# Gated layers: a tile's values moved to the step after its weights' transposes, ahead of the first scores

## The chip, the cores and the metric

The kernel runs on one core of a Trainium2 chip. The metric is the device time of one execution in microseconds (us). All times in this document are microseconds unless they are marked ns. The core has five engines with a queue of instructions each: TensorE (PE, with its weight loads shown apart as PEld), VectorE (DVE), ScalarE (ACT), GpSimd (POOL) and SyncE (SP), which here only issues DMA transfers. An engine takes its instructions in the order of its queue, and an instruction that waits for a semaphore holds up all that stand behind it.

## The reference

Two sequences of 2048 tokens with 256 features pass through four layers, each added to the stream. The second one, `_L0_ffn_ref`, is the one that matters here: two gated layers of local attention and a gated feed-forward part (FFN). Cut to its core:

```python
def _layer(x, wqkv, qs, ksc, wo, lg, lb, w1, b1, w2, b2):
    h = shift_token(x)                     # second half of the features from the token before
    q, k, v = split(h @ wqkv)              # 8 heads of 64
    q, k = l2norm(q) * qs, l2norm(k) * ksc
    q, k = rotary_xpos(q, k)
    o = local_attention(q, k, v)           # windows of 128: own window and the one before, masked
    x = x + o @ wo
    h = layernorm(shift_token(x)) * lg + lb
    a, g = split(h @ w1 + b1)              # 2 x 682
    return x + (a * gelu(g)) @ w2 + b2
```

## The kernel before

The kernel has three stages, each of which goes over all 4096 tokens: the first attention layer with its own FFN (to about 665 us), the gated layers (about 665 to 2140), and the last stage (to the end). The change touches the second stage only.

**Tiles and groups.** In the gated stage the residual stream `R` lies in SBUF for all tokens. A tile is 128 tokens; there are `NT` = 32 tiles, and four of them (`GT`) make a group of 512 tokens, of which there are 8 (`NG`). Attention goes by tiles, the FFN by groups, and there are `BL` = 2 layers.

**What one tile does** (class `Tile`). Each of these is a method, named as in the source, with the lines at which the profile shows it:

- `project` (matmuls L679) forms q, k and v of the tile in three calls. For q and k, ACT copies the product out of PSUM (`raw`, L689) and squares it (L690), and POOL forms one half of the rotation (`u2`, L695 and L698). For v, ACT copies it (L686).
- `norms`: DVE sums the squares (L710), POOL takes a maximum (L711) and the power -0.5 (`rn`, L713).
- `rotate_mul` and `rotate_add`: DVE forms the other half of the rotation (L718), adds both (L722), and for k multiplies by `rn` (L724).
- `to_features` (transposes L731, ACT copy L733) turns q or k so that the features lie on partitions.
- `scores` (32 matmuls L748, for half of the heads): DVE adds the mask and takes the maximum while it moves the scores out of PSUM (L757), and forms the exponents' shift (L764).
- `exponents` (ACT L775) and `normalise` (DVE L783, L786) make the weights.
- `weights_to_keys` (transposes L795 and L803) turns the weights of one half of the heads. The result goes to SBUF as `PT`, by ACT for half 0 (L799) and by DVE for half 1 (L797), and the rest as `PR` by ACT (L806).
- `swap_values`: two DMAs on SP make `vs`, the tile's v with its halves of 64 rows exchanged. `values` needs it in the matmuls that take `PR`, and the tile after needs it as `prev_vs`.
- `values` (matmuls L820 with `PT`, L832 with `PR`): the product leaves PSUM as `oT`, half by ACT (L840), half by DVE (L841).
- `output` (matmuls L847): DVE adds the product to `R` (L850).

**What one group does** (class `Ffn`). `shifted` issues the DMAs that make `sh`, the second half of the features of `R` moved down by one token; they wait for the `R` of the group's last tile. `normalise` is the layer norm: DVE statistics of `R` (L881) and of `sh` (L882), their aggregate (L883), POOL's variance and power (L93, L95), and eight DVE operations that write `h` (L887). `to_features` transposes `h` (L117, ACT L122), and POOL adds a bias to `R` (L895) and in the last layer a saved input (L899). `hidden` is one of six blocks of the hidden layer (L908, or L917 for the narrow sixth; ACT gelu L921; DVE L922). `output` is the product of one tile of the group (L929) with DVE's addition to `R` (L933). `begin_b` transposes a finished group of `R` for the projections of the layer (L653, ACT L654).

**The order.** The steps are written by hand. `at(step, what, ...)` puts work into a step, and a loop over the steps calls the methods in one fixed order. A tile projects in step t, has its scores in step t + 1 and, before the change, the part named "attend" in step t + 2: `weights_to_keys`, `values` and `output`. So one step holds three tiles: `p` (projects), `q` (scores) and `a` (attends). Three places in the step, `fill[0]` to `fill[2]`, take FFN work of an earlier group: three hidden blocks in each of two steps, then two outputs in each of two steps. Group g's FFN is prepared in step 4(g + 1) + 2 of its layer. PE runs its instructions nearly in the written order. For DVE, ACT, POOL and SP a scheduler may exchange instructions that do not depend on one another, so their queues differ from the written order. PSUM has eight banks that are given out in a ring.

Of the kernel before, what the change touches and what calls it, by code (L numbers as in the profile page):

```python
# [19 lines left out]
NT = NB * SEQ // P  # L20
TPS = SEQ // P
GT = 4
# [23 lines left out]
def kernel(ctx: ExitStack, tc: tile.TileContext, I: dict, out: bass.AP):  # L46
# [86 lines left out]
    def load_qkv(l):  # L133
        w = {}
        w["wqkv"] = T(wB, [P, KC, 3 * BIN], "wqkvB")
        load(w["wqkv"], I["L0_ffn_wqkv"][l].rearrange("(k p) n -> p k n", p=P))
        return w

    def load_wo(l):
        w = {}  # L140
        w["wo"] = T(wB, [P, BIN // P, D], "woB")
        load(w["wo"], I["L0_ffn_wo"][l].rearrange("(k p) n -> p k n", p=P))
        return w

    def load_ffn(l):
        w = {}
        for name in ("ln_g", "ln_b"):
            w[name] = T(wB, [P, KC], name + "B")
            load(w[name], I["L0_ffn_" + name][l].rearrange("(k p) -> p k", p=P))
        w1 = I["L0_ffn_w1"][l].rearrange("(k p) n -> p k n", p=P)  # L150
        w["w1"] = T(wB, [P, KC, 2, 5 * P], "w1B")

        w["w1r"] = T(wB, [P, KC, P], "w1rB")
        nc.gpsimd.memset(w["w1r"], 0.0)
        for h in range(2):
            load(w["w1"][:, :, h, :], w1[:, :, h * BHID : h * BHID + 5 * P])
            r0 = 64 * (1 - h)
            load(w["w1r"][:, :, r0 : r0 + BREM], w1[:, :, h * BHID + 5 * P : (h + 1) * BHID])
        b1 = I["L0_ffn_b1"][l]
        w["b1"] = T(wB, [P, 2, BNC], "b1B")  # L160
        for h in range(2):
            load(w["b1"][:, h, 0:5], b1[h * BHID : h * BHID + 5 * P].rearrange("(k p) -> p k", p=P))
            load(
                w["b1"][0:BREM, h, 5:6],
                b1[h * BHID + 5 * P : (h + 1) * BHID].rearrange("(k p) -> p k", p=BREM),
            )
        w2 = I["L0_ffn_w2"][l]
        w["w2"] = T(wB, [P, BNC, D], "w2B")
        load(w["w2"][:, 0:5, :], w2[0 : 5 * P].rearrange("(k p) n -> p k n", p=P))
        nc.gpsimd.memset(w["w2"][:, 5, :], 0.0)  # L170
        load(w["w2"][0:BREM, 5, :], w2[5 * P : BHID])
        w["b2"] = T(wB, [P, D], "b2B")
        load(w["b2"], bcast_rows(I["L0_ffn_b2"][l], D))
        return w


    with ExitStack() as st_a:
# [284 lines left out]
        def at(step, what, *args):  # L462
            steps.setdefault(step, {}).setdefault(what, []).append(args)
# [5 lines left out]
        for g in range(NG):  # L469
            at(GT * g - 2, "load", g)  # L470
            at(GT * g - 1, "begin", g)
            s = GT * (g + 1) + 2
# [7 lines left out]
        groups, tiles, ffns, done = {0: first_group}, {}, {}, None  # L480
        for s in range(min(steps), max(steps) + 1):
            todo = steps.get(s, {})
            p = a = f = n = q = None
# [3 lines left out]
            if s == GT:  # L487
                weights = {**load_qkv(0), **load_wo(0), **load_ffn(0)}
            if "project" in todo:
                (t,) = todo["project"][0]  # L490
                p = tiles[t] = TileA(t, groups[t // GT])
            if "scores" in todo:
                q = tiles[todo["scores"][0][0]]
            if "attend" in todo:
                a = tiles[todo["attend"][0][0]]
            fill = [lambda x=x: ffns[x[0]].output(x[1]) for x in todo.get("outputs", ())]
            fill += [lambda x=x: ffns[x[0]].hidden(x[1]) for x in todo.get("hidden", ())]
            fill = {0: [], 2: [fill[0:1], fill[1:], []], 4: [fill[0:2], fill[2:3], fill[3:4]]}[len(fill)]
            fill = fill or [[], [], []]
# [84 lines left out]
    with ExitStack() as st_b:  # L584
# [47 lines left out]
        def load_tab(g, sv):  # L632

            tab = T(wb, [P, 4, GT, BHD], "tab")
            t0 = g % GPS * GT
            load(tab, I["rope_b"][:, :, t0 : t0 + GT, :])
            nc.gpsimd.tensor_mul(tab, tab, sv.unsqueeze(2).to_broadcast([P, 4, GT, BHD]))
            return tab
# [304 lines left out]
        for l in range(BL):  # L943
            s0 = l * (NT + GAP)
            for t in range(NT):
                at(s0 + t, "project", l, t)
                at(s0 + t + 1, "scores", l, t)
                at(s0 + t + 2, "attend", l, t)
                if t % GT == 0:
                    at(s0 + t - 2, "tables", l, t // GT)  # L950
                    at(s0 + t - 1, "begin", l, t // GT)
            for g in range(NG):
                s = s0 + GT * (g + 1) + 2
                at(s, "prepare", l, g)
                for c in range(BNC):
                    at(s + 1 + c // 3, "hidden", l, g, c)
                for tt in range(GT):
                    at(s + 3 + tt // 2, "outputs", l, g, tt)
            at(s0 + NT - 1, "free_qkv", l)
            at(s0 + NT + 1, "free_wo", l)  # L960
            at(s0 + NT + 5, "free_ffn", l)

        wts = {0: weights}
        scales = [load_scales(l) for l in range(BL)]
# [1 line left out]
        groups, tiles, ffns = {}, {}, {}  # L966
        sh = None
        for s in range(min(steps), max(steps) + 1):
            todo = steps.get(s, {})
            p = a = q = None  # L970
            if "project" in todo:
                l, t = todo["project"][0]
                if l == BL - 1 and t == GT:
                    load_weights_c()
                p = tiles[l, t] = Tile(l, t, wts[l], tabs[l, t // GT], *groups[l, t // GT], tiles.get((l, t - 1)))
            if "scores" in todo:
                q = tiles[todo["scores"][0]]
            if "attend" in todo:
                a = tiles[todo["attend"][0]]
            fill = [lambda x=x: ffns[x[0], x[1]].output(x[2]) for x in todo.get("outputs", ())]  # L980
            fill += [lambda x=x: ffns[x[0], x[1]].hidden(x[2]) for x in todo.get("hidden", ())]
            for l, g in todo.get("tables", ()):
                tabs[l, g] = load_tab(g, scales[l])
            if "prepare" in todo:
                l, g = todo["prepare"][0]
                f = ffns[l, g] = Ffn(l, g, wts[l])
                sh = f.shifted(sh)
            fill += [lambda: None] * (3 - len(fill))

            if q:  # L990
                q.scores(0)
            if p:
                p.project(0)
            if q:
                q.exponents(0)
            if p:
                p.project(1)
            if q:
                q.scores(1)
            if p:  # L1000
                p.norms()
                p.rotate_mul(0)
                p.project(2)
            if q:
                q.exponents(1)
                q.normalise(0)
            if a:
                a.weights_to_keys(0)
            if p:
                p.rotate_add(0)  # L1010
            fill[0]()
            if a:
                a.weights_to_keys(1)
            if p:
                p.rotate_mul(1)
                p.rotate_add(1)
            if q:
                q.normalise(1)
            fill[1]()
            if a:  # L1020
                a.values()
                a.prev = None
            if q:
                q.swap_values()
            if "prepare" in todo:
                f.normalise()
            if p:
                p.to_features(0)
            fill[2]()
            if p:  # L1030
                p.to_features(1)
            if a:
                a.output()
                tiles.pop((a.l, a.t - 1), None)
            if "prepare" in todo:
                f.to_features()
            for l, g in todo.get("begin", ()):
                groups[l, g] = begin_b(g, groups[l, g - 1][1] if g else None)
            for (l,) in todo.get("free_qkv", ()):
                if l + 1 < BL:  # L1040
                    wts[l + 1] = load_qkv(l + 1)
            for (l,) in todo.get("free_wo", ()):
                if l + 1 < BL:
                    wts[l + 1].update(load_wo(l + 1))
            for (l,) in todo.get("free_ffn", ()):
                if l + 1 < BL:
                    wts[l + 1].update(load_ffn(l + 1))
# [303 lines left out]
```

## Time and profile before

| | us |
|---|---|
| median of 3 runs | 3002.23 |
| lowest and highest | 3000.06 and 3003.87 |
| the profiled execution, own time | 2999.28 |
| its span in the profile | 2997.1 |
| mean granted TensorE clock of it | 0.966 of full speed |
| gated stage, about | 665 to 2140 in the span |

A line of a group or of a wait names the engine, the operation's output and its source line; "L820 <- DVE PT L797" says that the instruction at line 820 waited for the instruction of DVE at line 797 that wrote `PT`. In a timeline a line has the start, the duration, the engine and line, the operation with its shapes, how many of its kind stand together, and in square brackets the idle time before it with what ended it. One group of the first layer, 1001.14 to 1087.36, took 86.22 us, with PE busy for 83.82 of them; one of the second layer, 1564.63 to 1653.50, took 88.87, with PE busy for 84.04.

### The profile page before, as it was taken

What the parts mean: (1) busy time and instruction counts of PE and PEld (TensorE: products, weight loads), DVE (VectorE), ACT (ScalarE), POOL (GpSimd) and SP (SyncE); (2) the same over time, 40 slices, a digit from 0 to 9 for tenths busy, and PEclk for the clock granted to TensorE, in tenths of its full rate; (3) what the DMA queues carried; (4) which work ended last, traced back from release to release, by engine and by line L of the source; (5) the groups of instructions that cost most, each with busy time, mean ns of one, the idle gap of its engine ahead of it and who ended that gap; (6) DMA issues with size and microseconds to landing.
All of it is one profiled execution on the core that took longest, in us unless ns stands there. A gap on an engine that the chain in (4) does not pass through costs nothing.

```text
span 2997.1 us, 50570 instructions
## 1 busy us (share of the span) xinstructions
PE 2738.9 (91%) x20146; PEld 1669.5 (56%) x20146; DVE 1680.5 (56%) x4457; ACT 1150.3 (38%) x2445; POOL 960.3 (32%) x935
## 2 busy tenths in 40 slices
PE   5788888886899999999999999999999999899998
PEld 3555566663566666665656666566544445444554
DVE  6676676634666566665556566555553334643333
ACT  2444444434555555655455555555230000210000
POOL 4443444324433343433344343333410012400001
PEclk8899999998999999999999999999999999999999
DMA  5000000002100101010101101101100000000000
GB/s 153 14 27 26 28 21 19 21 17 72 26 15 23 26 19 26 22 47 24 51 26 29 33 24 25 29 19 26 52 22 0 8 8 7 22 7 4 7 6 13
DMA packets 72763, 78.17 MB, mean 26 GB/s; under 512 B 18685, under 2 KB 57936, under 8 KB 72528
## 3 DMA queue, kind: packets, MB, share of 16 engines
q1 hardware_dynamic: 72528, 74.94, 8.9%
q8 instruction: 159, 2.61, 0.4%
q14 instruction: 76, 0.62, 0.1%
HBM read 42.50 MB, written 8.40 MB: 17 GB/s over the span
## 4 chain that ended last, share of the span: by engine, by line
PE 44%; DVE 18%; POOL 17%; issue 12%; ACT 6%; DMA 2%; SPq 0%; POOLq 0%; ACTq 0%; DVEq 0%
PE ps L1249 14%; POOL rn L713 6%; PE ps L1171 3%; PE ps L908 3%; PE ps L847 3%; DVE S L757 2%; PE ps L447 2%; PE ps L1195 2%; DVE ss L710 2%; POOL u L695 2%; PE ps L1161 2%; POOL S L365 2%; PE ps L439 2%; PE ps L679 2%; POOL rs L95 1%
## 5 line engine op out<-in xcount | busy, mean ns | idle before, releaser
L1249 PE MATMUL ps<-V,s 128*128 128x512 f32 x1024 | 468.3, 593 | 3.2 <-DVE s L1181 3.2
L775 ACT ACTIVATE S<-S,shift,rn 128x192 f32<-128x192 f32 x512 | 274.4, 539 | 168.4 <-DVE shift L764 168.0
L1249 PEld LDWEIGHTS ps<-V,s 128*128 128x128 f32 x1024 | 190.6, 190 | 226.4 <-issue 220.5
L908 PE MATMUL ps<-hT,w1B 128*128 128x512 f32 x640 | 290.3, 598 | 0.6 <-ACT hT L122 0.6
L695 POOL TENSOR_TENSOR u<-raw,tab 128x256 f32<-128x256 f32 x128 | 115.6, 903 | 488.5 <-ACT raw L689 488.4
L679 PE MATMUL ps<-wqkvB,za 128*128 128x512 f32 x384 | 211.9, 634 | 6.1 <-ACT za L654 6.1
L1204 POOL TENSOR_SCALAR veC<-mvC 128x1 f32<-128x1 f32 x32 | 16.6, 517 | 601.4 <-DVE mvC L1202 601.4
L365 POOL TENSOR_TENSOR S<-S,mxA 128x1024 f32<-128x1024 f32 x64 | 121.4, 1897 | 259.1 <-DVE mxA L364 222.8
L1177 DVE SCALAR_TENSOR_TENSOR s<-ps,strip 128x512 f32<-128x512 f32 x128 | 88.4, 691 | 206.8 <-PE ps L1171 206.8
L1192 ACT COPY oCT<-ps 128x512 f32<-128x512 f32 x32 | 18.8, 586 | 466.6 <-PE ps L1190 466.6
L679 PE MATMUL ps<-wqkvB,zb 128*128 128x512 f32 x384 | 197.8, 597 | 0.0
L713 POOL TENSOR_TENSOR rn<-ss,mhalf 128x16 f32<-128x16 f32 x64 | 195.6, 3057 | 5.3
L908 PEld LDWEIGHTS ps<-hT,w1B 128*128 128x128 f32 x640 | 117.4, 193 | 120.2 <-issue 115.1
L757 DVE CUSTOM_DVE_ANT_0 S<-ps,maskB 128x192 f32<-128x192 f32 x512 | 151.5, 351 | 47.0 <-PE ps L748 45.4
L929 PE MATMUL ps<-w2B,hh 128*128 128x256 f32 x768 | 175.5, 379 | 0.0
L439 PE MATMUL ps<-hT,wf 128*128 128x512 f32 x256 | 131.7, 650 | 25.5 <-DVE oT L404 20.2
L929 PEld LDWEIGHTS ps<-w2B,hh 128*128 128x128 f32 x768 | 141.6, 190 | 17.8 <-issue 0.7
L718 DVE TENSOR_TENSOR u<-raw,tab 128x512 f32<-128x512 f32 x128 | 90.7, 709 | 97.6 <-ACT raw L689 95.1
L722 DVE TENSOR_TENSOR u<-u,u 128x512 f32<-128x512 f32 x128 | 92.5, 723 | 88.2 <-POOL u L698 85.9
L786 DVE TENSOR_SCALAR S<-S,rdB 128x192 f32<-128x192 f32 x512 | 138.5, 326 | 2.2
L847 PE MATMUL ps<-woB,oT 128*128 128x256 f32 x512 | 131.1, 395 | 6.5 <-DVE oT L841 5.3
L748 PEld LDWEIGHTS ps<-qkT,qkT 64*64 64x64 f32 x4032 | 99.9, 135 | 65.0 <-issue 63.5
(210 smaller groups left out, 5462.2 us busy)
## 6 DMA issues: line engine op xcount, KB each, us to landing
vs<-v SPq DMA_DIRECT2D x128, 128.0 KB, 2.3
tab<-in_rope_b_dram SPq DMA_DIRECT2D x16, 512.0 KB, 3.9
xg<-in_L_attn_x_dram SPq DMA_DIRECT2D x8, 512.0 KB
xr<-in_L_attn_x_dram SPq DMA_DIRECT2D x8, 512.0 KB, 6.8
xs<-xr SPq DMA_DIRECT2D x8, 512.0 KB, 2.7
h<-xs SPq DMA_DIRECT2D x8, 512.0 KB, 3.6
rc<-in_rope_c_dram SPq DMA_DIRECT2D x8, 512.0 KB, 4.0
out_dram<-R SPq DMA_DIRECT2D x32, 128.0 KB, 1.7
```

The costliest lines, as they stand in the source:

```text
L365: nc.gpsimd.tensor_sub(Sh, Sh, mc.unsqueeze(2).to_broadcast([P, 2 * AG, P]))
L439: nc.tensor.matmul(pm, wf1[:, k, c * P : (c + 1) * P], self.hT[:, k, :], start=k == 0, stop=k == KC - 1)
L679: nc.tensor.matmul(pm, src[:, cols], self.w["wqkv"][:, k, part * BIN : (part + 1) * BIN], start=k == 0, stop=k == 1,)
L695: nc.gpsimd.tensor_mul(u2[:, :, 0:hd2], x[:, :, hd2:BHD], sin[:, :, 0:hd2].to_broadcast([P, BH, hd2]))
L713: nc.gpsimd.tensor_tensor(self.rn, ss, mhalf, ALU.pow)
L757: nc.vector.tensor_tensor_reduce(S[:, e, jj, :], sc[e][:, jj * KW : (jj + 1) * KW], self.mask[:, jj, :], 1.0, -3.0e38, ALU.add, ALU.max, t ...
L775: nc.scalar.activation(S[:, e, jj, :], S[:, e, jj, :], AF.Exp, bias=self.shift[half][:, a : a + 1], scale=self.rn[:, head : head + 1], acc ...
L786: nc.vector.tensor_scalar_mul(S[:, e, jj, :], S[:, e, jj, :], rd[:, a : a + 1])
L847: nc.tensor.matmul(pm[:, 0:D], self.oT[:, k, :], wo[:, k, :], start=k == 0, stop=k == BIN // P - 1)
L908: nc.tensor.matmul(pm, w["w1"][:, k, half, c * P : (c + 1) * P], hT[:, k, :], start=k == 0, stop=k == KC - 1,)
L929: nc.tensor.matmul(pm[:, 0:D], hh[:, c, tt * P : (tt + 1) * P], self.w["w2"][:, c, :], start=c == 0, stop=c == BNC - 1,)
L1249: nc.tensor.matmul(acc[i], s2[:, i * P : (i + 1) * P], self.V[:, J, :], start=J == 0, stop=J == TPS - 1,)
```

## The change

"attend" is split in two. `weights_to_keys` stays in step t + 2 ("weights"), and `values` and `output` go to step t + 3 ("values"), so that a step now holds four tiles: `p`, `q`, `a` and `o`. `values` of tile `o` is written at the head of the step, directly ahead of `scores(0)`; its `output` follows `fill[0]`. Both calls of `weights_to_keys` now stand together behind `fill[0]`, the output and `rotate_add(0)`; before, `fill[0]` stood between them. `swap_values` moves from the end of step t + 1 to the head of step t + 2. Since a group's `R` is finished one step later, the FFN's preparation, hidden blocks and outputs are put one step later too, and the loads of the second layer's weights move by one step (`free_wo`) and by two (`free_ffn`). "tables" and "begin" stay where they were, so that the preparation of a group now shares its step with a `begin_b`, where before `begin_b` shared one with the first three hidden blocks. The amount of arithmetic is the same.

```diff
--- before.py
+++ after.py
@@ -945,20 +945,21 @@
             for t in range(NT):
                 at(s0 + t, "project", l, t)
                 at(s0 + t + 1, "scores", l, t)
-                at(s0 + t + 2, "attend", l, t)
+                at(s0 + t + 2, "weights", l, t)
+                at(s0 + t + 3, "values", l, t)
                 if t % GT == 0:
                     at(s0 + t - 2, "tables", l, t // GT)
                     at(s0 + t - 1, "begin", l, t // GT)
             for g in range(NG):
-                s = s0 + GT * (g + 1) + 2
+                s = s0 + GT * (g + 1) + 3
                 at(s, "prepare", l, g)
                 for c in range(BNC):
                     at(s + 1 + c // 3, "hidden", l, g, c)
                 for tt in range(GT):
                     at(s + 3 + tt // 2, "outputs", l, g, tt)
             at(s0 + NT - 1, "free_qkv", l)
-            at(s0 + NT + 1, "free_wo", l)
-            at(s0 + NT + 5, "free_ffn", l)
+            at(s0 + NT + 2, "free_wo", l)
+            at(s0 + NT + 7, "free_ffn", l)
 
         wts = {0: weights}
         scales = [load_scales(l) for l in range(BL)]
@@ -967,7 +968,7 @@
         sh = None
         for s in range(min(steps), max(steps) + 1):
             todo = steps.get(s, {})
-            p = a = q = None
+            p = a = q = o = None
             if "project" in todo:
                 l, t = todo["project"][0]
                 if l == BL - 1 and t == GT:
@@ -975,8 +976,10 @@
                 p = tiles[l, t] = Tile(l, t, wts[l], tabs[l, t // GT], *groups[l, t // GT], tiles.get((l, t - 1)))
             if "scores" in todo:
                 q = tiles[todo["scores"][0]]
-            if "attend" in todo:
-                a = tiles[todo["attend"][0]]
+            if "weights" in todo:
+                a = tiles[todo["weights"][0]]
+            if "values" in todo:
+                o = tiles[todo["values"][0]]
             fill = [lambda x=x: ffns[x[0], x[1]].output(x[2]) for x in todo.get("outputs", ())]
             fill += [lambda x=x: ffns[x[0], x[1]].hidden(x[2]) for x in todo.get("hidden", ())]
             for l, g in todo.get("tables", ()):
@@ -987,6 +990,11 @@
                 sh = f.shifted(sh)
             fill += [lambda: None] * (3 - len(fill))
 
+            if o:
+                o.values()
+                o.prev = None
+            if a:
+                a.swap_values()
             if q:
                 q.scores(0)
             if p:
@@ -1004,12 +1012,14 @@
             if q:
                 q.exponents(1)
                 q.normalise(0)
+            fill[0]()
+            if o:
+                o.output()
+                tiles.pop((o.l, o.t - 1), None)
+            if p:
+                p.rotate_add(0)
             if a:
                 a.weights_to_keys(0)
-            if p:
-                p.rotate_add(0)
-            fill[0]()
-            if a:
                 a.weights_to_keys(1)
             if p:
                 p.rotate_mul(1)
@@ -1017,11 +1027,6 @@
             if q:
                 q.normalise(1)
             fill[1]()
-            if a:
-                a.values()
-                a.prev = None
-            if q:
-                q.swap_values()
             if "prepare" in todo:
                 f.normalise()
             if p:
@@ -1029,9 +1034,6 @@
             fill[2]()
             if p:
                 p.to_features(1)
-            if a:
-                a.output()
-                tiles.pop((a.l, a.t - 1), None)
             if "prepare" in todo:
                 f.to_features()
             for l, g in todo.get("begin", ()):
```

## The prediction

> **What bounds the kernel now.** I read the page first, then the waits of the gated stage, then two steps in the timeline. All times are us.
>
> ```profile
> span 2997.1 us, 50570 instructions
> PE 2738.9 (91%) x20146; PEld 1669.5 (56%) x20146; DVE 1680.5 (56%) x4457; ACT 1150.3 (38%) x2445; POOL 960.3 (32%) x935
> L713 POOL TENSOR_TENSOR rn<-ss,mhalf 128x16 f32<-128x16 f32 x64 | 195.6, 3057 | 5.3
> ```
>
> TensorE (PE) works 91% of the span, so only its idle time can be won. The diff touches the gated stage alone (about 740 to 2130), where the view of waits says what PE waited for:
>
> ```profile
> PE ps L820 <- DVE PT L797: 52.8, 51, 3.2
> DVE st L882 <- DMA sh<-R: 23.4, 15, 3.0
> PE ps L847 <- DVE oT L841: 5.3, 12, 0.7
> ```
>
> Columns: total, number, longest. The first row is the target: the values' second half (L820) waits for the copy of the transposed weights out of PSUM (L797, on DVE). The timeline says why, in a step with outputs 0 and 1:
>
> ```profile
> 1120.51 3.05 POOL L713 TENSOR_TENSOR rn<-ss,mhalf 128x16 f32<-128x16 f32 x1
> 1123.60 0.69 DVE L724 TENSOR_TENSOR u<-u,rn 128x512 f32<-128x512 f32 x1 [1.66 <-POOL rn L713]
> 1124.21 0.68 DVE L797 COPY PT<-ps 128x512 f32<-128x512 f32 x1
> 1124.94 0.69 PE L820 MATMUL ps<-PT,v 128*64 128x64 f32 x16 [1.10 <-DVE PT L797]
> ```
>
> L797's input was ready at 1120.4, but it stands on DVE behind L724, and L724 waits for POOL's power (3.05). So the wait is the projected tile's norm chain, passed to another tile's values by DVE's order.
>
> Last, the step in which a group's FFN is prepared:
>
> ```profile
> 1042.82 0.42 DVE L850 TENSOR_TENSOR R<-ps,R 128x256 f32<-128x256 f32 x1 [2.27 <-PE ps L847]
> 1043.27 1.67 SPq L56 DMA_DIRECT2D sh<-R  x2
> 1043.66 0.36 DVE L757 CUSTOM_DVE_ANT_0 S<-ps,maskB 128x192 f32<-128x192 f32 x1 [0.42 <-PE ps L748]
> 1046.43 0.49 DVE L882 BATCH_NORM_STATS2 st<-sh 128x6 f32<-128x128 f32 x2 [1.38 <-DMA sh<-R]
> 1050.04 1.04 POOL L95 TENSOR_TENSOR rs<-ve,mhalf 128x4 f32<-128x4 f32 x1
> ```
>
> From L850's end (1043.24) to the shifted rows' first use (1046.43) it is 3.19: SP's issue and the transfer. The scores' L757 stands ahead of that wait.
>
> **The change part by part.** A full group is four steps; I call them by their filler: H1 and H2 (hidden blocks), O1 (outputs 0, 1), O2 (outputs 2, 3, and the FFN's preparation). There are 12 full groups in the two layers (22 or so us a step).
>
> *Removed: the wait at L820.* Values now run at the head of the next step. L797 may end as late as that: 17.1 after O1's first L748, against 16.8 now worked out (below). Its rows: 0.32 + 1.10 + 0.57 = 2.0 in the layer-0 group from 1001 (and 0.41 at L847); in the layer-1 group from 1565, 1.10 + 0.62 + 2.05 + 0.32 = 4.1, and 0.74 at L847. Over all full steps the L820 waits come to 41.6 with the layers' boundary; some 8 of the 52.8 sit in the light steps at the stage's start, which a chain L748 to L724 of 13.7 bounds, and stay. With L847 (5, since output now has L748, six L679 and a filler ahead of it) and the drain at the end (some 2.5 to 4): **50.5 removed**.
>
> *What is late next.* The norm chain now ends at L731 for k, which needs L724. On PE an O1 step is: L748 0.83, L679 3.63, L748 0.83, L679 1.82, filler L929 2.65, L847 1.85, two transposes 1.3, filler 2.65, first L731 0.45: it reaches k's L731 at 16.0. L724 ends at 14.8 (as at 1109.46 before: 14.14 to 14.83). Margin 1.1: no wait. In H1 and H2 the fillers are longer (k's L731 at 21; L724 by 12.5, or 17.3 where POOL's L899 comes first): none.
>
> *O2 is another matter.* In the order of the changed program's DVE queue, in every full group, the FFN's block stands directly behind O1's L797: L882, L933, L883, L882 x2 and so on to five L887, then L841, three L887, and only then L757 of O2's scores. In before these were strewn through the step, behind L757. From O1's first L748: L724 ends 14.8; one L786; L850 ends 15.4; L797 16.8; L882 starts 15.4 + 3.19 = 18.6; statistics to 20.8 (they ran 3.2 with other work in between, about 2.2 alone); L93 and L95 1.44: 22.25; five L887 (0.34) and L841: 24.0; three L887: L757 at 24.7. O2's own L748 is at 18.35, so L757 starts 6.35 into its step, not 0.95: **5.4 late**. Then, by the durations of before: L764 7.7, last square 12.0, L710 to 14.4 (DVE has L722 and the second L757 between), L711, L713 14.85 to 17.9, L724 to 18.65. PE reaches k's L731 at 15.97. Wait 2.7 (2.4 to 3.15 by how L710 is placed); the 5.4 shrinks since the step had 1.1 of margin and, without the table load of O1, 1.6 more. With about 0.35 for values behind L797 and L933: **3.05 per O2**.
>
> POOL's L895 (2.39) is now ahead of O2's u2; raw comes at 10 to 11, so it is covered by L757's lateness, and costs up to 2.4 on L722 if that were gone. SP's queue has the shifted rows' issues (1.67) ahead of the tile's vs pair (1.1) where the pair came first; vs is read 20 later, by L832, so nothing, but 2.8 is what it would cost if vs were read at once. The two transposes standing together: their PSUM banks come from eight in a ring, the second needs the bank of the project read by the squares at 12.0, PE reaches it at 12.3: nothing, with 0.3 of cover; beyond it the same lateness costs one for one. ACT's copies of PR and PT, and the later loads of weights (one and two steps): nothing, 5 or more of margin; one more late step would cost what it waits.
>
> *The clock.* What does PE do after a wait of 3?
>
> ```profile
> 795.90 1.12 PE L820 MATMUL ps<-PT,v 128*64 128x64 f32 x16 [2.72 <-DVE PT L797]
> 1451.35 1.12 PE L820 MATMUL ps<-PT,v 128*64 128x64 f32 x16 [3.23 <-DVE PT L797]
> 790.00:800.00 10.00, 6.76 (x88) 5.49 (x87) 9.75 (x36) 4.84 (x14) 5.98 (x6) 0.79 0.06 13
> ```
>
> After 2.72 and after 3.23 the same L820 took 1.12, not 0.69, and the granted clock of the ten us (the third from the end of the row) was 0.79, where full groups show 1.00. What follows such a wait ran slow for one spell, 1.4 to 1.7 dearer; of eight waits of 2.0 to 2.5, two did that. The Trainium skill (TensorE: Matmul & The Clock Gate, "HAM oscillation — how this bites in real kernels") asks for no PE idle gap over about 3.4; by it a wait of 2.7 to 3.05 costs nothing more. The trace disagrees at 2.72, and decides: I take 1.4 per O2. With the rule the sum would be 17 lower.
>
> *Second rule.* The 3.19 carries O2's lateness. The skill (DMA: Bandwidth & Descriptors, the two cost components) gives a fixed 2.0 or so per transfer; by it L757 would be 1.2 earlier, the wait 1.5, the clock whole, and an O2 would cost 1.85. But here two issues queue on SP, and the 3.19 is measured on this very pair, so I keep it.
>
> *Ends of the stage.* Values and FFN end one step later: one more light step, +2.5 (it has 16 to 18, of which most held the drain's work before). At the layers' boundary a new wait of about 3.3 for L841 and h takes the place of 1.66 at L731 and 2.30 at L117: nothing; from −2 to +3.
>
> **Sum.** −50.5 + 12 × (3.05 + 1.4) + 2.5 = −50.5 + 53.4 + 2.5 = +5.4. On the profiled execution (2999.28; span 2997.1, 2.2 around it) this is 3004.7; the median stands 2.95 above that execution, so 3007.6, said as **3008**. An O2 must cost less than 4.0 for a gain. One fifth of a per cent (6 us) is about what a measurement of this kernel tells from no change; the forecast stands at that bound, on the slower side.
>
> **The rivals.**
> 1. *Faster: the FFN block is short enough.* If the shifted rows land in 2.0, or DVE's statistics fill the wait so that L757 is under 4 late, O2's wait is at most 1.5 and the clock stays whole: −50.5 + 12 × 1.85 + 2.5 = −26, 2976. If O2 waits for nothing, −48, 2954. For: the clock rule, the DMA rule, and that waits of 2 in the trace mostly left the clock alone. Against: the row at 1046.43 and the DVE order. It decides from an O2 cost of 4.0 downward.
> 2. *Slower, by more: the delay is not shrunk.* L757's 5.4 reach L731 nearly whole, because the second scores' L757, L710 and L722 also queue behind each other: 5.4 and 1.5 of slow clock are 6.9 per O2, −50.5 + 83 + 2.5 = +35, 3037. For: DVE in O2 is nearly full already (9.13 of 10 busy from 1050 to 1060). Against: the first chain had 2.7 of slack.
> 3. *It does not do what it says.* L797 stays behind L724, so the wait for POOL's power may just move from L820 to k's L731. If O1's margin of 1.1 were not there, 12 × 1.1 = +13 more: 3021. Against: values and output (3.8) no longer stand where they were, and 1.85 of output and 1.3 of transposes still lie ahead of L731.
>
> **How the numbers follow.** As computed, O2 costing 3.3 to 5.3 (−8 to +16, 2994 to 3019): 0.45, of which 0.06 is faster, 0.16 within the bound, 0.23 slower. Rival 1: 0.28 (0.26 faster, 0.02 within). Rival 2: 0.20, slower. Rival 3: 0.07, slower. Together 0.32 faster, 0.18 the same, 0.50 slower. The likeliest case's own range is 2994 to 3019; the range for 8 in 10 takes in most of rivals 1 and 2: 2974 to 3036.
>
> **What would show it.** Right: the row L820 <- L797 shrinks to about 8; a new row L731 <- L724 stands with some 12 waits of 2.4 to 3.2, all in steps with L117; in those DVE's L882 waits for sh<-R with L757 behind it, starting about 6 after L748; O1, H1 and H2 run without a wait over 0.3; after O2's wait L731 or its follower takes half as long again. Wrong: O2's L757 within 3 of its L748; waits at L731 in O1; or no slow matmuls after a wait of 3 (then the sum is −11, faster).

## The result, and the profile after

The changed kernel takes 3008.55 us (median of 8 runs, 3001.33 to 3012.32), the kernel before beside it 3002.01 (8 runs, 2998.51 to 3005.98). The ratio is 1.002, with a 95% interval of 1.0008 to 1.0033: slower by a fifth of a per cent, where 3008 was forecast. The profiled execution of the changed kernel took 3012.32, some 4 us more than the median, so its span is compared with care: the two profiled executions differ by 13, the medians by 6.5. The page's first lines:

```profile
span 3010.5 us, 50610 instructions
...
PE 2727.0 (91%) x20146; PEld 1687.9 (56%) x20146; DVE 1703.0 (57%) x4457; ACT 1148.4 (38%) x2441; POOL 962.4 (32%) x935
```

PE is busy for 12 us less, by the profile's model of its ends, and the span is 13 longer: more idle time. The waits of the gated stage (740 to 2130; total, number, longest):

```profile
PE ps L731 <- DVE rdB L783: 57.5, 19, 5.3
...
DVE st L882 <- DMA sh<-R: 30.4, 14, 3.5
...
PE ps L795 <- ACT sq L690: 13.1, 12, 2.1
...
PE ps L653 <- DVE PT L797: 9.1, 6, 2.3
...
PE ps L820 <- DVE PT L797: 3.7, 2, 2.1
```

The row that the change was to remove, L820 <- L797, is down from 52.8 to 3.7. In its place stands L731, the transposes of the rotated k: twelve of its waits, of 2.69 each, stand in the twelve steps with outputs 2 and 3 that prepare an FFN, and the other seven (2.8 to 5.3) in the light steps, those without outputs or hidden blocks, at the stage's start and at the layers' boundary. The profile names L783 as releaser because that tiny operation ends last; what L731 reads is written by L724, directly ahead of it on DVE. Here is one step that prepares an FFN (O2 of the prediction) in the timeline of the changed kernel. Its first L748 is at 1068.06, and the next step's at 1096.12.

```profile
1068.77 0.29 DVE L882 BATCH_NORM_STATS2 st<-sh 128x6 f32<-128x128 f32 x1 [1.93 <-DMA sh<-R]
...
1072.10 0.35 DVE L887 TENSOR_SCALAR h<-R,mv,rs 128x128 f32<-128x128 f32 x1 [1.48 <-POOL rs L95]
...
1074.39 2.39 POOL L895 TENSOR_TENSOR R<-R,b2B 128x1024 f32<-128x1024 f32 x1 [2.33 <-DVE h L887]
...
1074.48 0.35 DVE L757 CUSTOM_DVE_ANT_0 S<-ps,maskB 128x192 f32<-128x192 f32 x1
...
1075.71 1.09 DVE L764 SCALAR_TENSOR_TENSOR shift<-top,rn 128x4 f32<-128x4 f32 x1
...
1076.90 0.55 ACT L775 ACTIVATE S<-S,shift,rn 128x192 f32<-128x192 f32 x1 [8.19 <-DVE shift L764]
...
1080.03 0.69 DVE L722 TENSOR_TENSOR u<-u,u 128x512 f32<-128x512 f32 x1 [1.30 <-POOL u L698]
...
1081.11 0.66 PE L795 MATMUL ps<-ident,S 128*128 128x128 f32 x4 [0.85 <-ACT sq L690]
...
1087.30 0.69 DVE L724 TENSOR_TENSOR u<-u,rn 128x512 f32<-128x512 f32 x1 [1.07 <-POOL rn L713]
...
1088.13 0.63 PE L731 MATMUL ps<-ident,u 128*128 128x128 f32 x4 [2.69 <-DVE rdB L783]
...
1088.60 1.56 PE L117 MATMUL ps<-ident,h 128*128 128x128 f32 x8
...
1088.91 2.65 DVE L786 TENSOR_SCALAR S<-S,rdB 128x192 f32<-128x192 f32 x2
...
1089.07 2.38 POOL L637 TENSOR_TENSOR tab<-tab,sv 128x1024 f32<-128x1024 f32 x1 [1.81 <-DVE R L850]
...
1092.41 1.11 PE L653 MATMUL ps<-ident,R 128*128 128x128 f32 x4 [1.41 <-DVE PT L797]
```

DVE waits for the shifted rows, then for the norm's power, and the scores' L757 behind them starts 6.42 after its L748. Next, the tiny L764 lasts 1.09 beside POOL's L895, and ACT's exponents (L775) wait for it. The lateness runs down the chain to L724 and stops PE three times, at L795, L731 and L653. What follows here runs at a slow clock: L117 takes 1.56 where it took 1.04.

By steps, from one first L748 to the next (read in the timeline): the steps H1, H2 and O1 of the changed kernel take 22.96, 21.25 and 17.84, almost always without a wait over 0.3 (H1, which follows O2, took 23.6 to 24.5 in three groups). The O2 steps take 24.5 to 28.6, on average 26.83 over the ten between 890 and 1996, where their work without waits is 19.78 (an estimate: O1's 17.84 and 1.94 for L117 and L653; in experiment 8 such a step without waits takes 19.59). Five groups of the first layer take 16.4 longer than before (3.3 each), five of the second 3.6 less (0.7 each). Together that is 12.8 of the 13.4 by which the profiled span grew.

### The profile page after: what moved, and what is told of

It is laid out like the page before. It is cut to its first block, busy times and chain, and to the rows that moved or that the text cites. A ratio compares the mean times of both kernels' runs of the same rounds, so it can differ in the third digit from the quotient of the medians.

```text
span 3010.5 us, 50610 instructions
## 1 busy us (share of the span) xinstructions
PE 2727.0 (91%) x20146; PEld 1687.9 (56%) x20146; DVE 1703.0 (57%) x4457; ACT 1148.4 (38%) x2441; POOL 962.4 (32%) x935
## 5 line engine op out<-in xcount | busy, mean ns | idle before, releaser
L775 ACT ACTIVATE S<-S,shift,rn 128x192 f32<-128x192 f32 x512 | 274.3, 538 | 247.6 <-DVE shift L764 247.2
L695 POOL TENSOR_TENSOR u<-raw,tab 128x256 f32<-128x256 f32 x128 | 124.0, 969 | 513.2 <-ACT raw L689 513.2
L908 PE MATMUL ps<-hT,w1B 128*128 128x512 f32 x640 | 287.4, 593 | 0.4 <-ACT hT L122 0.4
L679 PE MATMUL ps<-wqkvB,za 128*128 128x512 f32 x384 | 213.8, 639 | 5.9 <-ACT za L654 5.9
L679 PE MATMUL ps<-wqkvB,zb 128*128 128x512 f32 x384 | 197.9, 597 | 0.0
L713 POOL TENSOR_TENSOR rn<-ss,mhalf 128x16 f32<-128x16 f32 x64 | 195.5, 3055 | 5.2
L908 PEld LDWEIGHTS ps<-hT,w1B 128*128 128x128 f32 x640 | 117.9, 190 | 131.0 <-issue 123.4
L757 DVE CUSTOM_DVE_ANT_0 S<-ps,maskB 128x192 f32<-128x192 f32 x512 | 151.5, 350 | 22.9 <-PE ps L748 22.9
L731 PE MATMUL ps<-ident,u 128*128 128x128 f32 x512 | 80.2, 286 | 92.7 <-DVE rdB L783 57.5
L786 DVE TENSOR_SCALAR S<-S,rdB 128x192 f32<-128x192 f32 x512 | 159.2, 362 | 2.2
L722 DVE TENSOR_TENSOR u<-u,u 128x512 f32<-128x512 f32 x128 | 90.0, 703 | 89.6 <-POOL u L698 86.7
L731 PEld LDWEIGHTS ps<-ident,u 128*128 128x128 f32 x512 | 63.8, 147 | 129.7 <-issue 63.2
```

What stands on the lines that cost most here:

```text
L679: nc.tensor.matmul(pm, src[:, cols], self.w["wqkv"][:, k, part * BIN : (part + 1) * BIN], start=k == 0, stop=k == 1,)
L695: nc.gpsimd.tensor_mul(u2[:, :, 0:hd2], x[:, :, hd2:BHD], sin[:, :, 0:hd2].to_broadcast([P, BH, hd2]))
L713: nc.gpsimd.tensor_tensor(self.rn, ss, mhalf, ALU.pow)
L731: nc.tensor.transpose(pt[:, j, :], self.u1[part][:, 2 * j : 2 * j + 2, :], ident)
L757: nc.vector.tensor_tensor_reduce(S[:, e, jj, :], sc[e][:, jj * KW : (jj + 1) * KW], self.mask[:, jj, :], 1.0, -3.0e38, ALU.add, ALU.max, t ...
L775: nc.scalar.activation(S[:, e, jj, :], S[:, e, jj, :], AF.Exp, bias=self.shift[half][:, a : a + 1], scale=self.rn[:, head : head + 1], acc ...
```

## The experiments

All ratios are to the kernel before, run on the same chip; its medians there were 2999.83 to 3002.22. The edits are shortened. After the first experiments the line numbers of some kernels are one or a few higher; the names are the same.

**1. The norm behind the scores on DVE.** The scheduler is told to queue the FFN's norm behind the first shift. (`issue_after(x)` queues what it encloses behind x on the engine of x, without a wait for its end.)

```diff
+            first = q.last            # L764 of scores(0)
...
-                f.normalise()
+                with tc.issue_after(first):
+                    f.normalise()
```

> The changed kernel, with the layer norm of a group's FFN queued on DVE behind the first shift (L764) of its own step; nothing else is changed. Theory (the norm block standing ahead of the scores' L757 makes the step with outputs 2 and 3 late): L757 starts within 3 us of L748 there, the wait at the second L731 falls from 2.69 to under 1, that step goes from 27 to about 21.5, twelve times, so about 2945 us; some of it may come back as a wait of L117 for the last L887. Rival (the late end of the norm chain comes from POOL, L895 and the power, and the place on DVE does not matter): the wait at L731 stays above 2 and the time within 10 us of 3008.

Measured: 2979.08, ratio 0.9933 (0.9918 to 0.9948). The waits at L731 in the full steps are gone, and so are those at L795; but:

```profile
PE ps L117 <- DVE h L887: 37.5, 28, 3.2
...
PE ps L731 <- DVE rdB L783: 27.6, 8, 4.9
```

Nine of the twelve steps now wait 3.0 to 3.2 at L117 and three 1.6, since five of the eight L887 came to stand behind L797. (The L731 row is that of the light steps at the stage's start and its boundary.) So the order on DVE is the cause of the wait at L731, and half of the expected 64 came back as the wait that the expectation named.

**2. Without the shifted copy.** `sh` becomes a view of `R`: the DMAs are left out, and with them the FFN's token shift.

```diff
-                load(sh[1:113, :, :], Rg[0:112, :, P:D])  ...
+                self.sh = Rg[:, :, P:D]
```

> The changed kernel without the shifted copy: the FFN's norm reads the second half of R in place, so the DMAs sh<-R and the wait for them are left out (the token shift of the FFN is not computed). Theory (the transfer's 3.3 us is half of L757's lateness of 5.4 or so): L757 about 3 us earlier in the step with outputs 2 and 3, no wait at L731 over 0.5, none at the second L795, clock whole there, 12 x 4.5 = 54 less, so about 2954 us. Rival (the norm block's own work on DVE and POOL, 6 us, is enough to hold the scores up): the wait at L731 stays above 1.5, about 2990 us.

Measured: 2971.66, ratio 0.9907 (0.9892 to 0.9923), between the two. The wait at L731 is 0.87 to 1.14 instead of 2.69, that at L795 is gone, and O2 takes 21.39 in three groups and 23.5 to 25.0 in the others: there L820 still waits 2.0 for L797. So the transfer is worth some 35 us in this order of DVE, and the block's own work still holds the scores up a little.

**3. PE kept busy in the wait, twice.** Six, then three extra matmuls ahead of the second L731.

```diff
+            if p and "prepare" in todo:
+                pm = bank()
+                for _ in range(6):          # 3 in the second kernel
+                    nc.tensor.matmul(pm, ident, p.za, start=True, stop=True)
```

> The changed kernel with six extra matmuls of 128x512 (about 2.6 us of PE, result not used) ahead of the second L731 of each step that prepares an FFN, so that PE works where it waited 2.69. Theory of the clock (a wait of 2.7 to 3 costs 1.4 us more by a half-granted clock): wait at L731 near zero, L117, L653 and L820 after it at full speed, the granted clock of that stretch from 0.66 back to near 1.00, 12 x 1.4 = 17 less: about 2991 us. Rival (the rule of 3.4 us: such a wait costs nothing beyond itself): no change, 3008, or 2 to 5 more by the matmuls that overshoot.

> As the run with six extra matmuls, but with three: the six took 5.2 us, twice the wait of 2.69 that they were to fill, so three take 2.6. Theory of the clock: in the changed kernel the stretch from the second L731 to the next L748 takes 8.0 us after the wait, and 4.7 with PE kept busy, of which 0.8 is a shorter wait at L653; so 2 to 2.5 us in each of twelve steps are clock, and the time falls to about 2982 us. Rival (a wait under 3.4 us costs only itself): within 5 us of 3008.

Measured: 3010.58, ratio 1.0039 (1.0025 to 1.0052), and 3016.39, ratio 1.0045 (1.0028 to 1.0063). Both miss. Six took 5.2, twice what had been reckoned, so PE came to L731 later than it had by waiting; what followed ran at full speed. Windows over the same stretch (the figure after POOL's is the granted clock), of the kernel with six matmuls:

```profile
1085.00:1090.00 5.00, 5.00 (x15) 2.29 (x13) 3.89 (x8) 2.26 (x7) 3.35 (x2) 1.00 0.32 105
1090.00:1096.00 6.00, 5.43 (x118) 4.63 (x117) 3.18 (x7) 3.38 (x6) 1.24 (x2) 1.00 0.01 3
```

and of the changed kernel:

```profile
1085.00:1090.00 5.00, 2.31 (x18) 2.01 (x16) 3.79 (x10) 3.68 (x9) 3.19 (x2) 0.91 0.34 105
1090.00:1096.00 6.00, 4.59 (x65) 3.75 (x67) 2.69 (x4) 2.02 (x4) 1.63 (x2) 0.51 0.00 0
```

So in this step the clock falls after the wait and does not fall where PE was kept busy; in the kernel with six matmuls it falls behind none of the twelve L731. With three matmuls the wait only moved: L653 then waits 2.1 to 2.3 for L797 (nine such waits, 20 us). Behind four of the nine the clock was slow again (L820 takes 1.98 at 1100.62), behind five it was not (1.15 at 1190.92). As a price of the clock the three-matmul run says nothing.

**4. The table's multiplication elsewhere.** On POOL, L637 is queued behind the second u2 (L698) of a hidden step (H2), and so ahead of that step's L711 and L713.

```diff
-                    at(s0 + t - 2, "tables", l, t // GT)
+                    at(s0 + t - 3, "tables", l, t // GT)
...
+                with tc.issue_after(p.last_u2):
+                    tabs[l, g] = load_tab(g, scales[l])
```

> The changed kernel with the multiplication of the rotation table (POOL, L637, 2.4 us) moved from the end of the step that prepares an FFN to the middle of a step with hidden blocks. Theory (while L637 runs, DVE's L786 x2 takes 2.65 instead of 0.5, so L797 behind it is late for L653 and L820, which costs the wait of 1.1 to 2.3 and slow clock): those waits go in the seven steps that show them, 2.5 each, about 2991 us. Rival (L797 is late because of L724 alone): the waits stay, within 5 us of 3008. The moved L637 delays L713 of its new step by 2.4, where L731 has 3.5 to spare.

Measured: 3010.92, ratio 1.003 (1.0021 to 1.0039): no gain, which is the rival's time. Yet the rival's reason is wrong: the waits at L653 and L820 that the move was aimed at are gone, and in this kernel (L731 is L732 here, L117 unchanged) the stretch reads:

```profile
1090.71 0.63 PE L732 MATMUL ps<-ident,u 128*128 128x128 f32 x4 [2.69 <-DVE rdB L784]
...
1091.17 1.71 PE L117 MATMUL ps<-ident,h 128*128 128x128 f32 x8
...
1091.48 0.54 DVE L787 TENSOR_SCALAR S<-S,rdB 128x192 f32<-128x192 f32 x2
...
1092.67 1.92 PE L654 MATMUL ps<-ident,R 128*128 128x128 f32 x8
...
1096.22 0.85 PE L749 MATMUL ps<-qkT,qkT 64*64 64x128 f32 x32
```

DVE's pair takes 0.54 with POOL idle, against 2.65 beside L637. The gain in O2 (some 25.5) is paid back in H2, which goes from 21.25 to 22.51: PE's L917 now waits 1.0 for L922, with L637 beside DVE's work there. DVE's tiny L764 (L765 here) lasts 2.30 beside it, and 0.16 otherwise. This run also gives the price of the clock alone, since no second wait follows L731: 1090.71 to 1096.22 is 5.51, and the same stretch with PE kept busy (1090.21 to 1094.88, less a wait of 0.57) is 4.10. The difference, 1.41, follows a wait of 2.69. One step of the same kernel has this wait and no slow clock behind it:

```profile
1634.92 0.63 PE L732 MATMUL ps<-ident,u 128*128 128x128 f32 x4 [2.69 <-DVE rdB L784]
...
1639.07 0.85 PE L749 MATMUL ps<-qkT,qkT 64*64 64x128 f32 x32
```

There the stretch takes 4.15, so the price within one kernel is 1.36.

**5. The kernel before, with L797 on ACT.** One line, no change of the schedule.

```diff
-                    nc.vector.tensor_copy(PT, pt)
+                    nc.scalar.copy(PT, pt)
```

> The kernel before, with the one copy L797 moved from DVE to ACT, so that it is not behind L724; the schedule is untouched. This prices what the change was to remove. Theory (each wait costs its idle time and about 0.3 more[...]): 45 us of idle and some 51 x 0.3 = 15 more go, about 2942 us. Rival one (the idle time only): about 2957. Rival two (ACT has its exponents ahead of the copy, so that the wait returns as L820 <- ACT): within 10 us of 3002.

Measured: 2972.03, ratio 0.9914 (0.9895 to 0.9933), 28 less than before; none of the three forecasts had it. The waits of its gated stage, with those under 1 us left out:

```profile
PE ps L731 <- DVE rdB L783: 16.7, 5, 3.9
...
PE ps L818 <- ACT PT L796: 14.4, 11, 3.6
...
PE ps L845 <- DVE oT L839: 9.3, 14, 1.0
...
PE ps L117 <- DVE h L885: 4.5, 3, 2.3
```

(L818 and L845 are the values and the output.) The 52.8 for L797 are down to 14.4, but some of the gain returns as other waits, as rival two had it: of 0.8 to 1.9 in a step of each second-layer group for the same copy on ACT, of 0.6 at the output, and of 3.9 at L731 in the light steps at the start, which take 19 to 21 us in place of 16 to 18. A step with outputs 0 and 1 takes 18.17, against 19.47 with a wait of 1.10: the wait cost its idle time and 0.2. The changed kernel's same step takes 17.84, so 0.33 more comes with the changed order of PE's work (the values' place, the output's, and the two `weights_to_keys` together; not taken apart).

**6. The norm put into DVE's order by hand.** The statistics behind L764, the eight L887 behind L710 and ahead of L724.

```diff
+                with tc.issue_after(first):      # L764 of scores(0)
+                    f.normalise()                # statistics, L93, L95
...
+                with tc.issue_after(p.red):      # L710
+                    f.apply()                    # eight L887
...
+                    with tc.issue_after(f.last):
+                        p.rotate_add(1)          # L724
```

> The changed kernel with the FFN's norm put by hand into DVE's order: the statistics behind the first shift (L764), the eight operations that write h behind L710 and ahead of L724, where DVE waits for POOL's power anyway. Theory: no wait at L731, L795 or L117 over 0.5 in these steps, which come down to 20 to 21 us: against the run with the norm merely behind L764 (2979) 3 us less in twelve steps, about 2940 us. Rival (DVE has no room there, so that L724 or L717 is late again): waits at L731 of 1 to 2, about 2965.

Measured: 2941.44, ratio 0.9794 (0.9778 to 0.981), as expected. O2 is down from 26.8 to 21.5, a little over the 20 to 21 expected of it. What is left in it, in the timeline of this kernel:

```profile
1069.09 2.44 POOL L898 TENSOR_TENSOR R<-R,b2B 128x1024 f32<-128x1024 f32 x1
...
1069.57 2.51 DVE L722 TENSOR_TENSOR u<-u,u 128x512 f32<-128x512 f32 x1
...
1073.49 0.63 PE L731 MATMUL ps<-ident,u 128*128 128x128 f32 x4 [0.88 <-DVE u L724]
```

(L898 is L895 of the changed kernel.) L722 took 2.51 beside POOL's addition, and 0.69 in the changed kernel's step shown above (1080.03), where POOL ran nothing long.

**7. A control: the same order of the norm in the kernel before.**

> The kernel before with the same hand-set order of the FFN's norm on DVE, and nothing of the change. A control: how much of the gain of the run with the norm split is the norm's order in itself. Theory (before, the norm was already spread behind the scores, so its order cost PE 1 us or so in a group): 2990 to 3003 us, so that the 60 us of that run come from the move of the values once the norm is out of the way. Rival (the norm's place was worth as much in the kernel before): under 2970 us.

Measured: 3015.16, ratio 1.004 (1.0031 to 1.005). By itself this order is worth nothing there, and costs 13, some 12 more than the top of the range expected: L731 waits for L724 in 19 places (37.4 us) and L820 still for L797 (40.3). Between the two profiled executions, which differ by 8, ten full groups make 5; one wait of 8.1 at L731 stands at the layers' boundary. The 60 us belong to the move of the values together with the norm's order, to neither alone.

**8. POOL's long operations moved, on top of 6.** First the table as in experiment 4, then all of them, then only the bias L895 (between the two halves of the next step).

> The run before this one and the moved table multiplication (L637) together. Theory: what L637 still costs in those steps goes too, 0 to 16 us under the run with the norm split, about 2930 us. Rival (once the norm chain is early, L637 no longer meets DVE work on the path): no difference to it.

> The run with the norm split, with POOL's two long operations on [128 x 1024] taken out of the places where DVE has work on the path: L637 (the table) between the two halves of a step with hidden blocks, L895 (the bias added to R, and L899 in the second layer) to the same place of the step after the preparation. In the run with the norm split, L722 took 2.51 instead of 0.69 beside L895, which gives the last wait at L731 (0.88), and L786 x4 took 3.13 beside L637 (the wait at L820, 0.65). Theory: both waits go, the step comes to 19.8 from 21.5, and no hidden block waits: 12 x 1.7 = 20 less than 2941, about 2921 us. Rival (the long operations cost the same wherever they stand, as when L637 alone was moved and a wait of 1.0 at L917 came up): within 6 us of 2941.

> The run with the norm split, with only POOL's addition of the bias (L895) moved between the two halves of the next step; the table (L637) stays where that run has it, and in the second layer the addition of the saved input comes ahead of the bias. When L637 and the two additions were all moved, the step with the preparation lost its waits (19.59), but the two hidden steps gained 1.2 and up to 1.7. Theory: L895 alone takes the wait at L731 (0.88) away in twelve steps and costs a hidden step 0.1: 12 x 0.8 = 9 less than 2941, about 2932 us. Rival (a wait of 1 comes up at L907 or L917): within 4 us of 2941.

```diff
+                with tc.issue_after(p.last_u2):   # u2 of q, in the step after
+                    added = late.bias()           # L895
+                with tc.issue_after(added):
+                    p.project(1)
```

Measured: 2949.2 (0.9821, 0.9806 to 0.9836), 2946.45 (0.9811, 0.9786 to 0.9836) and 2928.52 (0.9767, 0.9752 to 0.9781). The table in H2 takes O2 to 20.66 and H2 to 22.51, a loss that neither side had forecast. The run with all of them moved came out where the rival had it (the same cost elsewhere), 25 over the theory's 2921: O2 is at 19.59, its work without a wait, but H2 is at 22.44 and H1 of the second layer at 24.70, by waits of about 1 at L917 and L908 for L922. The bias alone, with the table left where it was, came out within 4 of the theory's 2932: O2 at 19.59, H2 at 21.25, and H1 0.1 longer in the first layer (1.4 in the second, where L918, a hidden block, waits about 1.0 in six places, the wait that the rival named). This is the fastest version of the study, 73 us under the kernel before.

**9. The place in the step, on top of 6.** The values behind `project(0)`.

```diff
-            if o:
-                o.values()        # ahead of scores(0)
...
                 p.project(0)
+            if o:
+                o.values()
```

> The run with the norm split, with the values behind the first projection instead of directly ahead of the first scores; all else is the same. It asks what the place at the head of the step is worth. Theory (values and scores are both matmuls on small tiles and follow each other without the 0.33 us that PE loses on the way from a large tile to a small one; and nothing stands between the first scores and the projections, which start the norm chain): 0.3 in some 44 steps is 14, and the chain starts 1.6 later, which the twelve steps that prepare an FFN pay in full or half (10 to 19): 2965 to 2975 us. Rival (only the step counts, not the place in it): within 6 us of 2941.

Measured: 2995.8, ratio 0.9984 (0.997 to 0.9998), 54 more than experiment 6. The direction was expected, but the time is 21 to 31 over the range of the theory. Each step is longer, O1 by 1.2. In the timeline of this kernel, the start of such a step:

```profile
1144.73 0.44 PE L748 MATMUL ps<-qkT,qkT 64*64 64x128 f32 x4
...
1145.10 1.13 PE L679 MATMUL ps<-wqkvB,za 128*128 128x512 f32 x2
...
1146.15 0.89 PE L748 MATMUL ps<-qkT,qkT 64*64 64x128 f32 x28
...
1146.97 1.13 PE L679 MATMUL ps<-wqkvB,zb 128*128 128x512 f32 x2
...
1148.02 1.15 PE L820 MATMUL ps<-PT,v 128*64 128x64 f32 x32
...
1149.73 1.12 PE L679 MATMUL ps<-wqkvB,za 128*128 128x512 f32 x2
```

and in kernel 6:

```profile
1120.35 0.60 PE L731 MATMUL ps<-ident,u 128*128 128x128 f32 x4
...
1120.88 1.15 PE L820 MATMUL ps<-PT,v 128*64 128x64 f32 x32
...
1122.47 0.85 PE L748 MATMUL ps<-qkT,qkT 64*64 64x128 f32 x32
...
1123.25 1.13 PE L679 MATMUL ps<-wqkvB,za 128*128 128x512 f32 x2
```

With the values ahead, they cover the time that ACT needs to copy the last transposes (L733) for the scores (without them, L748 waits 0.7 for that copy in four light steps), and the two groups of small matmuls stand together. Without them the scores come straight after L731; PE's order is cut up (four of the L748, two L679, the other 28), and there are more passages between large and small tiles. How the 1.2 divides between the cover and the passages was not separated.

## Why the prediction was right, and where its terms were off

*The mechanism* was right in its main steps. The waits for L797 went (52.8 to 3.7, where 8 were to stay in the light steps, which now wait at L731 instead). L757 starts 6.42 after L748, where 6.35 was worked out; L731 in O2 waits 2.69, where 2.7 was; O1, H1 and H2 of the full groups have almost no wait over 0.3. Experiments 1 and 6 show that DVE's order is the cause, and experiment 2 what the transfer's 3.2 contributes. (The section of the Trainium skill that the prediction cites for a fixed 2.0 per transfer, DMA: Bandwidth & Descriptors, "Two cost components", gives it for transfers that GpSimd issues; these two are issued by SyncE.) The agreement at L731 is in part luck: L724 ended 19.9 into the step, not 18.65, and PE, held up at L795, came to L731 at 17.4, not 15.97. Both waits start from the same late squares (L690), L795's directly and L731's by the chain from them to L724. So L731 waits 2.69 in all twelve O2 steps, while L795 waits from 0.8 to 2.1: what the scores are late beyond a point is paid at L795.

*The removed term was too small.* In the profile's rows the waits at L820 in full steps add up to 44.6 and not 41.6, which is 3 of it. Per group the steps without O2's waits now take 22.96 + 21.25 + 17.84 + 19.78 = 81.83, against 86.22 and 88.87 before: 4.4 and 7.0 less, where the waits' own lengths gave 2.4 and 4.8. The missing 2.0 to 2.2 are the restart after a wait (0.2, experiment 5) and the gain of 0.33 a step from PE's new order, which I had costed at nothing. Over twelve groups that is 25 us. In the second layer the five groups averaged 89.5 before, so that 7.7 went: in two of them the wait of 2.0 had a slow clock behind it, and the prediction counted only the waits' own lengths.

*The added term was too small by as much.* An O2 costs 26.83 − 19.78 = 7.05, not 4.45. The step of the working that failed first is the second pair of transposes, costed at nothing with 0.3 of cover: the squares ended 13.0 into the step rather than 12.0, and L795 waits 0.85, in some groups up to 2.1. The trace shows where that 1.0 comes from: in all twelve O2 steps L764 ends with POOL's L895, so that it lasts 1.1 where it took 0.16, and ACT's exponents and the squares behind them come that much later (from the first L775 to the last square's end it is 4.2 before and after). The prediction had L895 covered by L757's lateness. No run moved L895 with the rest unchanged, so what this alone costs was not measured. The second step is the 0.35 for the values behind L797. It did not see that POOL's L637 falls into this step in most groups and holds up DVE's L786 (the pair takes 2.65, not 0.5); seven steps wait 1.1 to 2.3 for L797 then, and the slow clock can last longer: in the step at 1068 the stretch after L731 takes 7.99, less 1.41 of wait is 6.58, against 4.10 at full clock, so 2.5 and not 1.4. Over twelve steps the term is 31 us short.

*The clock's term* had the right price for a fall, 1.41 and 1.36 after a wait of 2.69 (experiment 4) where 1.4 was taken, but not every such wait brings the fall. Behind the twelve waits of 2.69 at L731 the clock fell at once eight times, three times only behind a second wait of 2.1 to 2.3, and once not at all; behind the nine waits of 3.0 to 3.2 of experiment 1 it fell four times. In the kernel before, two of the seven waits of 2.0 to 2.5 at L820 had it. Windows of 6 us from the end of a wait (the clock is the third number from the end), two of the changed kernel, behind 2.69 each:

```profile
1000.55:1006.55 6.00, 6.00 (x108) 5.77 (x112) 2.71 (x9) 3.41 (x6) 2.63 (x2) 0.73 0.05 17
1991.77:1997.77 6.00, 5.84 (x118) 4.83 (x119) 3.62 (x14) 3.27 (x6) 0.82 (x1) 1.00 0.35 101
```

and two of experiment 1, behind 3.13 and 3.08:

```profile
1086.07:1092.07 6.00, 5.82 (x114) 4.61 (x115) 2.83 (x14) 2.78 (x5) 2.60 (x2) 1.00 0.15 34
1616.12:1622.12 6.00, 5.82 (x110) 5.18 (x110) 1.80 (x6) 2.88 (x5) 3.44 (x2) 0.72 0.30 90
```

What decides, the moment at which the wait falls or the work around it, no run separates. The Trainium skill (TensorE: Matmul & The Clock Gate, "HAM oscillation — how this bites in real kernels") would have had the clock whole up to some 3.4; the windows of experiment 3 show 0.51 in the stretch with the wait of 2.69 and 1.00 where PE was kept busy. Taking the row over the rule was right on the whole, and charging all twelve steps alike was not.

*So the sum was right because two errors of some 25 to 30 us cancelled*, and that is luck. Per group the forecast was +2.1 in the first layer and −0.4 in the second; measured were +3.3 and −0.7. In the first layer the O2 steps cost 7.6 each over their work, and the slow clock that runs into the next H1 0.1, against 4.5 saved; in the second 6.5 and 0.5, against 7.7 saved. The boundary and the ends of the stage come to some +0.6 and were not taken apart. By the two profiled executions the change costs 13, over twice the forecast's 5.4; by the medians it costs 6.5.

*The rivals.* The first (the FFN's block is short enough) did not happen, but it named the lever: with the block out of the way the same move of the values is worth 60 us, and 73 with the bias moved. The second had L724 later still and a cost of 6.9; the cost was 7.05 in the profile, by other ways: L724 was later than in the likeliest case, but PE was held up as much. The third (the wait only moves to k's L731) is wrong for three steps in four.

## What to carry to other kernels

A wait that is taken away by moving work to another step frees time only if the engine that made it late finds no other block at its head: read the changed program's order on that engine, and follow what now stands ahead of the next step's first instruction. Sum the clear steps and the late step by their own lengths from start to start, not by the waits listed; here each term was 25 to 30 us from the truth, and only their sum was right. When a long operation of another engine is moved, look at what runs beside it in its new place, as the table's multiplication cost a hidden step what it had cost the step before.

## What the runs showed of the hardware that was not expected

- Some DVE operations that started while POOL ran a [128 x 1024] addition or multiplication of 2.4 us lasted until POOL's had ended: a single L786 2.43 against 0.31 (7 of 7 beside L637 in the changed kernel, ending 0.12 after it), L722 2.51 against 0.69 (14 of 14 beside L898 in experiment 6, ending 0.55 after it), and the tiny L764 1.1 against 0.16 (12 of 12 beside L895 in the changed kernel). All of these read SBUF alone. Operations that read PSUM took their usual time there: 51 of L757 beside L895 0.35, twelve of L850 beside L898 0.41. So did the sum L710, which reads SBUF (1.21, 14 of 14 beside L637 in experiment 4). Where a held operation lay on PE's path it cost a wait of 0.7 to 2.3.
- After a wait of 2.69 the granted clock mostly fell: to 0.72 over the 6 us behind it in the kernel with the table moved, where the work took 1.4 more; with a second wait of 1.41 following, as in the changed kernel at 1088, it was 0.51 and 2.5. After one such wait in twelve, and after five of nine of 3.0 to 3.2 in experiment 1, it stayed at 1.00.
- A wait of PE costs about 0.2 beyond its idle time (1.30 for 1.10, experiment 5). A step whose values follow transposes and precede scores is 0.33 shorter than one whose values stand between outputs and transposes, with the same work; other places changed with them, so the cause of the 0.33 is not shown.
